# Differential attention in small blocks: steps of a pair spread over one round more, older pairs first

## The chip, the cores and the metric

The kernel runs on one core of one Trainium2 chip (trn2). It is one launch that computes a whole small network. The metric is the time of the program on the device, in microseconds (us); several runs are made, and the median is compared. A profiled execution of the same program gives the trace from which the views below come.

The engines are TensorE (PE, its weight loads are listed as PEld), VectorE (DVE), ScalarE (ACT), GpSimd (POOL) and SyncE (SP, which issues DMAs). They run side by side, each takes its own instructions in the order of the program, and they wait for each other at semaphores.

## The reference

The input is x, 2 sequences of 1024 tokens with 256 features, in float32. Eight residual layers follow each other:

```python
x = x + L0_attn_a(norm(x));  x = x + L0_ffn(norm(x))
x = x + L0_attn_b(norm(x));  x = x + L0_ffn(norm(x))
x = x + L1_attn_a(norm(x));  x = x + L1_ffn(norm(x))     # the stage of the change
x = x + L1_attn_b(norm(x));  x = x + L1_ffn(norm(x))
```

The stage of the change is the third pair. `L1_attn_a` is differential attention with 16 heads of 16 features, 4 key heads, and a softmax over the difference of two softmaxes:

```python
energy = einsum('bqhad,bkhad->bahqk', qd, kd)            # a = 0, 1
energy = where(causal, NEG, energy)
scores = softmax(energy / sqrt(D))
diff = scores[:, 0] - lam * scores[:, 1]
diff = softmax(where(causal, NEG, diff))
att = einsum('bhqv,bvhd->bqhd', diff, v)
att = att * rsqrt(mean(att * att) + EPS) * rms_w * (1 - LAM_INIT)
out = att.reshape(b, s, E) @ Wo
```

`L1_ffn` is a gated network of width 2048, `(gelu(x @ Wg.T) * (x @ Wu.T)) @ Wd.T`, with tanh gelu.

## The kernel before, in words

The function `attn_d_ffn1` computes this third pair of layers. The queries are taken in eight blocks of 128 tokens, i = 0 to 7, in both sequences (b = 0, 1). A causal block i has keys up to (i + 1) x 128. Blocks 0 to 3 have at most 512 keys and are called small, blocks 4 to 7 large. In each block and sequence the 16 heads are taken as eight pairs of heads. There are 8 x 2 x 8 = 128 pairs, the first 64 of them in small blocks.

A pair goes through these steps (functions in `attn_d_block`):

- `scores` (L1178): PE multiplies queries and keys, four matmuls into the two PSUM tiles `e` (two buffers, so one pair at a time; a large pair does it in two parts).
- `highest` (L1189): DVE adds the mask, writes the negated scores to SBUF tiles `p`, and takes the extreme value of each row into `nm`.
- `exponentials` (L1200): ACT takes exp in place with the row sums `sm`, four instructions.
- `ratio` (L1208, L1209 on DVE; L1213, L1217 on POOL): a reciprocal and a product on DVE, then POOL scales the second softmax and masks its diagonal block.
- `difference` (L1226 on DVE; L1229, L1230 on POOL): DVE adds the two and takes the row maximum `md`; POOL negates it and subtracts it.
- `turn` (L1237 on PE, L1241 on ACT), once for each head: PE transposes the blocks into the PSUM tile `dT` (one buffer), ACT takes the exp into `pT`.
- `weigh` (L1254), for every second pair: PE multiplies with the values into `py`; after the last pair of a block DVE transposes it (L1263).

The loop over rounds n in `attn_d_ffn1` starts pair n in round n, takes ratio and difference of pair n-1, the turn of pair n-2 and the weighing of pair n-3. The order within a round is written by hand: the engines PE, DVE, ACT and POOL keep the order in which the code issues (`in_order`).

Between these steps the round takes "fill" steps from the table `at`, in three portions. They are the inputs of the next block (layer norm stats, rows, turn; `queries`, `keys` and their transposes), the output of the last one (`squares`, `root`, `normalize`, `project`), and the feed-forward network (FFN) of the last block: stats, rows, turn, eight `gate` steps (L1387 on PE, a copy L1393 on ACT), `gelu` (L1398, one ACT instruction over 4096 columns), eight `up` steps (L1387, product L1395 on DVE) and eight `down` steps (L1404 on PE). For block i they fall, counted from round 16(i+1): squares 2, root 3, normalize 4, project and stats 5, rows 6, turn 7, gate 8 to 11, gelu 11, up 13 to 16, down 17 to 20. Queries and keys of the next block are made in round 12 for b = 0 and in round 15 for b = 1.

While blocks are small, `bank` alternates between two PSUM banks for gates, products and projections; in large blocks there is one.

Of the kernel before, what the change touches and what calls it, by code (L numbers as in the profile page):

```python
# [10 lines left out]
F32 = mybir.dt.float32  # L11
I32 = mybir.dt.int32
BF16 = mybir.dt.bfloat16
AF = mybir.ActivationFunctionType
# [7 lines left out]
P = 128  # L22
NTT = NT // P
NB = T // P
# [20 lines left out]
class Net:  # L45
# [899 lines left out]
    def attn_d_ffn1(self, w, wo, cos, sin, nlam, rms_w, deq):  # L945
# [5 lines left out]
        nc, tc = self.nc, self.tc  # L951
        NH, NKV, D = 16, 4, 16
        with ExitStack() as ctx:
# [33 lines left out]
            at, pairs = {}, []  # L987
# [4 lines left out]
            for i in range(NB):  # L992
                n = 16 * i
                tile_ = type("tile", (), {})()
                blocks = [
                    self.attn_d_block(pools, tile_, b, i, kT[b], v[b]) for b in range(B)
                ]
                for m, step in zip(
                    (-9, -8, -6, -4, -4, -2, -2, -2, -1, -1, -1, -1, -1),
                    (*self.attn_d_inputs(ps, work, tile_, i), *blocks[0][0], *blocks[1][0]),  # L1000
                ):
                    add(n + m if i else -1, step)
                for _, units in blocks:
                    pairs.extend(units)

                n += 16
                squares, root, normalize, project = self.attn_d_out(ps, work, tile_, wo, i)
                if i == NB - 1:

                    for m, step in enumerate((squares, root, normalize, project)):  # L1010
                        add(n + 2 + m, step)
                    continue
                stats, rows, turn, gate, gelu, up, down = self.ffn1_parts(ps, work, i, deq)
                for m, step in (
                    (2, squares), (3, root), (4, normalize), (5, project), (5, stats), (6, rows),
                    (7, turn), *((8 + k // 2, gate[k]) for k in range(8)), (11, gelu),
                    *((13 + k // 2, up[k]) for k in range(8)),
                    *((17 + k // 2, down[k]) for k in range(8)),
                ):
                    add(n + m, step)  # L1020
            nothing = type("nothing", (), {"large": False})()

            def pair(n):
                return pairs[n] if 0 <= n < len(pairs) else nothing

            def do(u, name, *args):
                f = getattr(u, name, None)
                if f:
                    f(*args)

            for step in at[-1]:
                step()
            for n in range(max(at) + 1):
                if n == 16 * 4:

                    self.ps.release()
                    self.ps = tc.alloc_tile_pool(name="d_ps1", bufs=1, space=PSUM)
                    self.small = False
                fill = at.get(n, [])
                k = (len(fill) + 2) // 3, (2 * len(fill) + 2) // 3  # L1040
                u, last, turned, weighed = (pair(n - j) for j in range(4))
                do(u, "scores", 0)
                do(u, "highest", 0)
                if not u.large:
                    do(u, "exponentials")
                do(weighed, "weigh")
                do(last, "ratio")
                for step in fill[: k[0]]:
                    step()
                do(turned, "turn", 0)  # L1050
                if u.large:
                    u.scores(1)
                    u.highest(1)
                for step in fill[k[0] : k[1]]:
                    step()
                do(turned, "turn", 1)
                if u.large:
                    u.exponentials()
                do(last, "difference")
                for step in fill[k[1] :]:  # L1060
                    step()
            self.ps.release()
# [22 lines left out]
    def attn_d_block(self, pools, tile_, b, qb, kT, v):  # L1085
# [52 lines left out]
        def pair(t, s):  # L1138
# [55 lines left out]
                if j == 1:  # L1194
                    nc.vector.tensor_tensor(own.nm, own.nm, nm, ALU.min)

            def exponentials():
                for h in range(2):
                    for a in range(2):
                        nc.scalar.activation(  # L1200
                            own.p[h][a], own.p[h][a], AF.Exp,
                            bias=own.nm[:, h, a : a + 1], scale=-1.0,
                            accum_out=own.sm[:, h, a : a + 1],
                        )

            def ratio():

# [24 lines left out]
            def turn(h):  # L1232
                dT = self.ps.tile(
                    [P, 512 if self.small else 1024], F32, tag="dT", name="dT"
                ).rearrange("p (n q) -> p n q", q=P)
                for kb in range(qb + 1):
                    nc.tensor.transpose(  # L1237
                        dT[:, kb, :], own.p[h][0][:, kb * P : (kb + 1) * P], self.ident
                    )
                pT = work.tile([P, NB, P], F32, tag="pT", name="pT", bufs=4)  # L1240
                nc.scalar.activation(pT[:, 0 : qb + 1, :], dT[:, 0 : qb + 1, :], AF.Exp)  # L1241
                shared[t, s + h] = pT

# [120 lines left out]
    def ffn1_parts(self, ps, work, i, deq):  # L1364
# [31 lines left out]

        def gelu():
            nc.scalar.activation(f.inter, f.inter, AF.Gelu_apprx_tanh)  # L1398

        def down(b, quarter):  # L1400
            if b == quarter == 0:
# [658 lines left out]
```

## Time and profile before

| what | value |
|---|---|
| median of 3 runs | 3041.03 us (3031.7 to 3042.51) |
| the profiled execution | 3038.91 us |
| its span, first to last instruction | 3037.2 us |
| busy over the span | PE 85%, DVE 64%, ACT 44%, POOL 34% |
| small blocks of the stage | 1066.8 to 1478.4 us |
| large blocks of the stage | 1478.4 to about 2174 us |
| PE busy in the small blocks, i = 0, 1, 2, 3 | 38.2, 75.0, 97.6, 106.1 us |
| mean granted TensorE clock | 0.901 |

The windows view gives the busy time of each engine in a stretch, and in brackets how many instructions started there. The wait view has one line for a pair of waiter and releaser: engine and line that waited, what it waited for, the total in us, how often, and the longest. In the timeline a line is the start, the length, the engine, the line of the code, the operation, what it writes and reads, and in square brackets the idle time before it and what ended it. A busy PE is not PE at its peak, because the ends of matmuls are modelled.

### The profile page before, as it was taken

How to read it: one execution, taken by the hardware profiler on the slowest of the kernel's cores; microseconds unless marked ns; L12 is line 12 of the kernel's file. 1: busy time of each engine (PE TensorE's matmuls, PEld its weight loads, DVE VectorE, ACT ScalarE, POOL GpSimd, SP SyncE). 2: the span in 40 equal slices, each digit the busy share in tenths (PEclk: the TensorE clock that was granted, in tenths of full speed). 3: DMA queues.
4: the chain of work that ended last, by engine and by line, in shares of the span. 5: the costliest groups of instructions: out<-in, count | busy, mean ns of one | idle time of the engine just before them, and what ended most of it. 6: DMA issues, size and time to landing. Idle time of an engine off the chain costs nothing.

```text
span 3037.2 us, 66929 instructions
## 1 busy us (share of the span) xinstructions
PE 2585.5 (85%) x26384; PEld 1608.0 (53%) x26384; DVE 1953.5 (64%) x6736; ACT 1324.4 (44%) x2672; POOL 1039.6 (34%) x1672
## 2 busy tenths in 40 slices
PE   6999998999988757887878878878777988898988
PEld 2333344434434434565655555555555767677777
DVE  5777665766664456667776858678656656566552
ACT  2776840454453256465564556656622112112110
POOL 3445232212114466566665646556500000000000
PEclk8999997999999867898989888898988889999999
DMA  3000000000001000000000000000001101101100
GB/s 115 1 1 1 1 1 1 1 1 1 1 17 40 28 1 1 1 1 1 1 1 1 1 1 1 1 1 1 18 17 24 24 20 20 23 11 36 24 9 14
DMA packets 61979, 35.39 MB, mean 12 GB/s; under 512 B 43216, under 2 KB 58080, under 8 KB 61664
## 3 DMA queue, kind: packets, MB, share of 16 engines
q1 hardware_dynamic: 59472, 29.49, 3.7%
q8 instruction: 208, 3.41, 0.4%
q10 hardware_dynamic: 2192, 1.61, 0.2%
q14 instruction: 107, 0.88, 0.1%
HBM read 22.68 MB, written 8.39 MB: 10 GB/s over the span
## 4 chain that ended last, share of the span: by engine, by line
PE 38%; DVE 13%; ACT 7%; issue 4%; POOL 3%; DMA 0%; POOLq 0%; ACTq 0%; DVEq 0%
PE ph L1387 6%; PE po L1894 5%; PE pg L1881 4%; ACT p L1200 4%; PE e L1178 4%; DVE p L1189 4%; PE pu L1881 4%; PE dT L1237 3%; PE po L1404 2%; DVE p L1226 2%; POOL p L1213 1%; PE py L1254 1%; PE pq L1564 1%; PE kh L1564 1%; PE pa L1564 1%
## 5 line engine op out<-in xcount | busy, mean ns | idle before, releaser
L1189 DVE CUSTOM_DVE_ANT_0 p<-e,mask 128x512 f32<-128x512 f32 (+3 forms) x768 | 381.6, 553 | 108.9 <-PE e L1178 107.7
L1200 ACT ACTIVATE p<-p,nm 128x128 f32<-128x128 f32 (+7 forms) x512 | 389.9, 764 | 97.4 <-DVE nm L1189 88.1
L1213 POOL TENSOR_SCALAR p<-p,ra,neg_lam 128x128 f32<-128x128 f32 (+7 forms) x256 | 221.8, 866 | 238.1 <-DVE ra L1209 178.6
L1237 PE MATMUL dT<-ident,p 128*128 128x128 f32 x1152 | 198.7, 306 | 114.4 <-ACT pT L1241 32.0
L1241 ACT ACTIVATE pT<-dT 128x128 f32<-128x128 f32 (+7 forms) x256 | 165.4, 646 | 283.5 <-PE dT L1237 282.2
L196 POOL TENSOR_SCALAR ln_mv<-ln_mv 128x2 f32<-128x2 f32 x56 | 17.6, 315 | 730.0 <-DVE ln_mv L194 720.0
L1178 PE MATMUL e<-kT,qT 32*128 32x512 f32 (+3 forms) x1536 | 235.4, 628 | 28.4 <-DVE nm L1189 27.0
L1226 DVE CUSTOM_DVE_ANT_0 p<-p,rs 128x128 f32<-128x128 f32 (+7 forms) x256 | 207.7, 832 | 70.1 <-POOL p L1217 69.8
L1237 PEld LDWEIGHTS dT<-ident,p 128*128 128x128 f32 x1152 | 153.5, 157 | 173.6 <-POOL p L1217 51.4
L845 ACT ACTIVATE pr<-s 128x512 f32<-128x512 f32 (+3 forms) x384 | 157.3, 497 | 162.9 <-PE s L840 154.2
L1230 POOL TENSOR_SCALAR p<-p,md 128x128 f32<-128x128 f32 (+7 forms) x256 | 208.8, 816 | 25.4
L550 ACT ACTIVATE pr<-s 128x1024 f32<-128x1024 f32 (+1 forms) x192 | 145.3, 812 | 131.3 <-PE s L544 83.7
L1894 PE MATMUL po<-down,inter 128*128 128x256 f32 x576 | 164.8, 451 | 3.4 <-issue 2.2
L805 PE MATMUL s<-kT,qT 32*128 32x512 f32 (+3 forms) x768 | 155.3, 518 | 3.8 <-DVE q_pad L813 1.9
L1881 PE MATMUL pg<-xT,gate 128*128 128x256 f32 x576 | 151.5, 409 | 6.5 <-ACT xT L225 5.5
L555 ACT ACTIVATE pr<-pr 128x1024 f32<-128x1024 f32 (+1 forms) x192 | 152.1, 852 | 0.0
L813 DVE CUSTOM_DVE_ANT_0 masked<-s,mask 128x128 f32<-128x128 f32 (+3 forms) x256 | 110.6, 487 | 58.9 <-PE s L805 58.8
L1894 PEld LDWEIGHTS po<-down,inter 128*128 128x128 f32 x576 | 129.8, 230 | 27.8 <-issue 2.3
L558 POOL TENSOR_SCALAR_AFFINE_SELECT pr<-pr 128x256 f32<-128x256 f32 x128 | 90.1, 721 | 154.7 <-ACT pr L555 57.7
L1881 PE MATMUL pu<-xT,up 128*128 128x256 f32 x576 | 139.3, 386 | 0.0
L1887 DVE TENSOR_TENSOR inter<-inter,pu 128x512 f32<-128x512 f32 x72 | 49.3, 685 | 133.9 <-PE pu L1881 133.9
L1387 PE MATMUL ph<-xT,gate 128*128 128x256 f32 x448 | 121.0, 417 | 10.3 <-ACT xT L225 10.1
(313 smaller groups left out, 5398.4 us busy)
## 6 DMA issues: line engine op xcount, KB each, us to landing
uk_d<-uk SPq DMA_DIRECT2D x128, 32.0 KB, 1.9
r<-uk_d SPq DMA_DIRECT2D x8, 512.0 KB, 3.9
x<-in_L_attn_a_X SPq DMA_DIRECT2D x4, 512.0 KB, 6.1
qh_d<-qh SPq DMA_DIRECT2D x8, 256.0 KB, 2.6
o<-qh_d SPq DMA_DIRECT2D x128, 16.0 KB, 1.7
out<-x SPq DMA_DIRECT2D x4, 512.0 KB, 3.1
w<-in_L_ffn_W2T SPq DMA_DIRECT2D x1, 1024.0 KB, 7.8
pk<-in_L_ffn_gate_packed SPq DMA_DIRECT2D x8, 128.0 KB, 2.4
```

What stands on the lines that cost most here:

```text
L845: nc.scalar.activation(pr[:, g, off:512], tiles[g][:, 0:m], AF.Exp, scale=0.25)
L1178: nc.tensor.matmul(own.tiles[h][:, a, 0 : hi - lo], made["q"][r : r + 32, a, t, :], kT[r : r + 32, a, lo:hi], start=True, stop=True,)
L1189: nc.vector.tensor_tensor_reduce(own.p[h][a][:, lo:hi], own.tiles[h][:, a, 0 : hi - lo], neg_row[:, T - nk + lo : T - nk + hi], -1.0, 3e38 ...
L1200: nc.scalar.activation(own.p[h][a], own.p[h][a], AF.Exp, bias=own.nm[:, h, a : a + 1], scale=-1.0, accum_out=own.sm[:, h, a : a + 1],)
L1213: nc.gpsimd.tensor_scalar(p1, p1, own.ra[:, h : h + 1], nlam[:, head : head + 1], ALU.mult, ALU.mult)
L1226: nc.vector.tensor_tensor_reduce(p0, p0, p1, own.rs[:, h, 0:1], -3e38, ALU.add, ALU.max, md)
L1230: nc.gpsimd.tensor_scalar(p0, p0, md, 1.0, ALU.add, ALU.mult)
L1237: nc.tensor.transpose(dT[:, kb, :], own.p[h][0][:, kb * P : (kb + 1) * P], self.ident)
L1241: nc.scalar.activation(pT[:, 0 : qb + 1, :], dT[:, 0 : qb + 1, :], AF.Exp)
L1387: nc.tensor.matmul(ph[:, j, :], w[:, kc, m * P : (m + 1) * P], f.xT[:, kc, :], start=(kc == 0), stop=(kc == 1),)
L1881: nc.tensor.matmul(ph[:, j, :], m_[:, kc, m * P : (m + 1) * P], f.xT[:, kc, :], start=(kc == 0), stop=(kc == 1),)
L1894: nc.tensor.matmul(f.po[:, b], inter[m // 2][:, m % 2, b * P : (b + 1) * P], wd[:, m % 2, (m // 2) * C : (m // 2 + 1) * C], start=(m == 0) ...
```

## The change

In small blocks (rounds 0 to 63) a pair's steps are spread over one round more: ratio of n-1, difference of n-2, turn of n-3, weighing of n-4. Within a round the order on every engine is: scores of n, difference of n-2, ratio of n-1, first turn of n-3, weighing of n-4, gelu if it is due, maxima and exponentials of n, half of the fill, second turn of n-3, the other half. Both heads of a pair share one `pT` tile. The FFN steps of blocks 0, 1 and 2 come one round later. In all blocks gelu is due one round later than that (12 instead of 11), and is issued after the first turn, apart from the other fill. The last small pair keeps the lags of the large ones. In large rounds the order is as before except for gelu.

```diff
                 stats, rows, turn, gate, gelu, up, down = self.ffn1_parts(ps, work, i, deq)
+                n += 1 if i < 3 else 0
                 for m, step in (
                     (2, squares), (3, root), (4, normalize), (5, project), (5, stats), (6, rows),
-                    (7, turn), *((8 + k // 2, gate[k]) for k in range(8)), (11, gelu),
+                    (7, turn), *((8 + k // 2, gate[k]) for k in range(8)), (12, gelu),
...
+            first_large = 16 * 4
+            ratios, differences, turns, weighings = {}, {}, {}, {}
+            for m, u in enumerate(pairs):
+                a, b = (2, 3) if m < first_large - 1 else (1, 2)
+                for steps, lag in (
+                    (ratios, 1), (differences, a), (turns, b), (weighings, b + 1)
+                ):
+                    steps.setdefault(m + lag, []).append(u)
...
-                fill = at.get(n, [])
-                k = (len(fill) + 2) // 3, (2 * len(fill) + 2) // 3
-                u, last, turned, weighed = (pair(n - j) for j in range(4))
-                do(u, "scores", 0)
-                do(u, "highest", 0)
-                if not u.large:
-                    do(u, "exponentials")
-                do(weighed, "weigh")
-                do(last, "ratio")
+                fill = [step for step in at.get(n, []) if not hasattr(step, "long")]
+                long = [step for step in at.get(n, []) if hasattr(step, "long")]
+                k = (len(fill) + 2) // 3, (2 * len(fill) + 2) // 3, (len(fill) + 1) // 2
+                u = pairs[n] if n < len(pairs) else nothing
+                if n < first_large:
+                    u.scores(0)
+                    do(differences, n, "difference")
+                    do(ratios, n, "ratio")
+                    do(turns, n, "turn", 0)
+                    do(weighings, n, "weigh")
+                    for step in long:
+                        step()
+                    u.highest(0)
+                    u.exponentials(0)
+                    u.exponentials(1)
+                    for step in fill[: k[2]]:
+                        step()
+                    do(turns, n, "turn", 1)
+                    for step in fill[k[2] :]:
+                        step()
+                    continue
+                if u.large:
+                    u.scores(0)
+                    u.highest(0)
+                do(weighings, n, "weigh")
+                do(ratios, n, "ratio")
                 for step in fill[: k[0]]:
                     step()
-                do(turned, "turn", 0)
+                do(turns, n, "turn", 0)
+                for step in long:
+                    step()
...
-                pT = work.tile([P, NB, P], F32, tag="pT", name="pT", bufs=4)
+                if large or h == 0:
+                    own.pT = work.tile([P, NB, P], F32, tag="pT", name="pT", bufs=4)
+                pT = own.pT if large else own.pT[:, 4 * h : 4 * h + 4]
...
+        gelu.long = True
```

More of the change, by code (lines that the diff above doesn't have):

```diff
@@ L1021, in attn_d_ffn1, with do @@
             nothing = type("nothing", (), {"large": False})()
[L1023 to L1029, printed above, removed]
+            first_large = 16 * 4
[6 more added lines that the diff above has]
+                    steps.setdefault(m + lag, []).append(u)
+            def do(steps, n, name, *args):
+                for u in steps.get(n, []):
+                    f = getattr(u, name, None)
+                    if f:
+                        f(*args)
             for step in at[-1]:
                 step()
-            for n in range(max(at) + 1):
-                if n == 16 * 4:
+            for n in range(max(max(at), max(weighings)) + 1):
+                if n == first_large:
                     self.ps.release()
@@ L1055, in attn_d_ffn1 @@
                     step()
-                do(turned, "turn", 1)
+                do(turns, n, "turn", 1)
                 if u.large:
-                    u.exponentials()
-                do(last, "difference")
+                    u.exponentials(0)
+                    u.exponentials(1)
+                do(differences, n, "difference")
                 for step in fill[k[1] :]:
@@ L1195, in highest, with exponentials @@
                     nc.vector.tensor_tensor(own.nm, own.nm, nm, ALU.min)
[L1197 to L1204, printed above, removed]
+            def exponentials(h):
+                for a in range(2):
+                    nc.scalar.activation(
+                        own.p[h][a], own.p[h][a], AF.Exp,
+                        bias=own.nm[:, h, a : a + 1], scale=-1.0,
+                        accum_out=own.sm[:, h, a : a + 1],
+                    )
             def ratio():
```

## Prediction

> **What bounds the kernel now.** I read the windows view first, cut at the rounds of the differential-attention stage (a round runs from the first scores matmul, L1178, of one pair of heads to that of the next). The 64 rounds of small blocks last from 1066.8 to 1478.4 us, 411.6 us; the four windows are the blocks i = 0 to 3, the fifth is the large blocks.
>
> ```profile
> core 0: us, PE busy (x) PEld busy (x) DVE busy (x) ACT busy (x) POOL busy (x), PEclk, DMA share, GB/s
> 1066.80:1131.70 64.90, 38.16 (x249) 22.07 (x248) 36.83 (x248) 36.77 (x165) 45.41 (x131) 0.61 0.00 1
> 1131.70:1230.80 99.10, 74.95 (x465) 48.69 (x465) 63.43 (x291) 57.29 (x181) 59.18 (x142) 0.77 0.00 1
> 1230.80:1346.30 115.50, 97.63 (x641) 67.42 (x640) 78.00 (x295) 67.59 (x180) 70.66 (x144) 0.85 0.00 1
> 1346.30:1478.40 132.10, 106.11 (x741) 71.12 (x740) 91.50 (x297) 77.19 (x180) 82.82 (x146) 0.90 0.00 1
> 1478.40:2174.00 695.60, 571.98 (x4368) 385.93 (x4369) 521.36 (x1718) 404.49 (x700) 404.33 (x557) 0.88 0.00 1
> ```
>
> No engine fills a window: POOL is the busiest at i = 0 with 45.4 of 64.9 us, PE after that with 75, 98 and 106 of 99, 116 and 132. Over the four the best engine leaves 65 + 99 + 116 + 132 - (45 + 75 + 98 + 106) = 88 us. The wait view of these 411.6 us says who waits:
>
> ```profile
> ACT p L1200 <- DVE nm L1189: 88.1, 59, 5.0
> DVE p L1226 <- POOL p L1217: 64.3, 74, 1.6
> POOL p L1213 <- DVE ra L1209: 59.7, 40, 4.6
> ```
>
> The second and third are one ring. The timeline of a round without other work (round 6, 1086.27 to 1089.80, 3.53 us) shows it:
>
> ```profile
> 1087.77 0.28 DVE L1189 CUSTOM_DVE_ANT_0 p<-e,mask 128x128 f32<-128x128 f32 x1
> ...
> 1087.98 0.17 DVE L1208 RECIPROCAL rs<-sm 128x4 f32<-128x4 f32 x1
> 1088.19 0.16 DVE L1209 TENSOR_TENSOR ra<-sm,rs 128x2 f32<-128x2 f32 x1
> ...
> 1088.53 0.44 POOL L1213 TENSOR_SCALAR p<-p,ra,neg_lam 128x128 f32<-128x128 f32 x1 [0.55 <-DVE ra L1209]
> 1089.05 0.29 POOL L1217 TENSOR_SCALAR_AFFINE_SELECT p<-p 128x128 f32<-128x128 f32 x1
> ...
> 1089.37 0.36 DVE L1226 CUSTOM_DVE_ANT_0 p<-p,rs 128x128 f32<-128x128 f32 x1 [1.02 <-POOL p L1217]
> ...
> 1090.28 0.35 DVE L1226 CUSTOM_DVE_ANT_0 p<-p,rs 128x128 f32<-128x128 f32 x1 [0.55 <-POOL p L1217]
> ```
>
> DVE finishes the maxima, makes the ratio, POOL scales and masks, and DVE waits 1.02 + 0.55 us for that before its difference and before the next round's maxima. DVE works about 1.9 us and POOL 2.63; neither runs beside the other for long, so the round takes 3.53.
>
> **What the Trainium skill says.** "Perfetto Trace Analysis", Identifying Performance Opportunities: take the most occupied engine of a regime, and ask what ends its gaps; matmul busy time is a poor measure for TensorE. The trace agrees: a full PE round (round 25, 4.73 us) shows PE busy 100% while lighter, starved ones also show high digits. "SBUF — State Buffer", Who interferes with whom: a VectorE instruction with two SBUF inputs contends with a GpSimd one that reads SBUF. The trace shows it: L1213 at 512 columns takes 0.76 us alone and 1.27 beside a difference (L1226), while L1226 keeps its 0.76. "TensorE: Matmul & The Clock Gate", Part 1: after an idle window of about 3.4 us the clock is halved. Here eight matmuls after a 5.26 us wait took 3.78 us against 1.99. "ScalarE: Activation LUTs", What ACT_TABLE_LOAD costs: 1283 ns a load, and the trace has 1.28.
>
> **The change part by part.** Counted by engine in the two programs, no instruction is added or removed: 14147 on PE, 6739 on DVE, 2179 on ACT with 18 table loads, 1678 on POOL, in each. No DMA is moved. So the sum is over order alone.
>
> Cost of a pair's steps, from the mean occupied time of their rows at i = 0, 1, 2, 3. DVE: maxima 0.85, 1.38, 1.91, 2.45; ratio 0.3 each; difference 0.70, 0.98, 1.20, 1.45. POOL: ratio (L1213, L1217) 1.54, 1.80, 2.07, 2.40; difference (L1229, L1230) 1.09, 1.35, 1.73, 2.06. ACT: exponentials 1.58, 2.02, 2.43, 2.85; pT 0.52, 0.72, 0.92, 1.11. PE: scores 0.52, 0.65, 0.90, 1.10; turn 0.30, 0.56, 0.84, 1.12; weigh, every second round, 0.40 to 1.0. Fill: each gate, up or down step 1.93 on PE with 0.5 ACT or 0.66 DVE; gelu 1.28 + 3.62 + 1.28 = 6.2 ACT; queries 0.9 PE, 0.9 DVE, 1.7 POOL; keys 0.4, 0.9, 1.1; root 2.7 and normalize 1.8 DVE; project 1.9 PE.
>
> I put each step into its round, before and after, and took the fullest engine of each round. Example: round 6 is POOL, 1.54 + 1.09 = 2.63 (measured 3.53). Round 25 (two gates) is PE, 0.65 + 0.56 + 2 x 1.93 = 5.07 (4.73: already full). Round 37 (project, stats) is DVE, 5.2, and took 10.08. Sums by block before: 48.9, 85.3, 102.9, 113.2 = 350, against the measured 411.6: **61 us are not work of the fullest engine**. About 40 lie in rounds without a gate, up or down step, 23 in those with one; the gelu pairs of rounds hold none. The same sums after: 47.8, 84.1, 103.5, 113.6 = 349. The shift of FFN steps by a round is thus free in work; what it can bring is the 61.
>
> 1. Difference two rounds behind, first on DVE and on POOL. In round n DVE takes the difference of n-2, whose mask POOL made in round n-1; POOL then has the md and p of n-2 to do while DVE makes the ratio of n-1. The ring is cut: POOL runs on without gap where it is fullest. A light round falls from 3.53 to about 2.7, 0.85 us for each of some ten at i = 0. Queued behind the difference on DVE are ratio and maxima; scores (0.5 to 1.1 us) run on PE beside them, so the maxima wait little.
> 2. Turn of n-3 right after the scores on PE, weigh of n-4 after it: their inputs are from earlier rounds, so PE's wait for POOL (48.8 + 25.4 + 24.3 us in the view) goes mostly. The pT tile for both heads lets two pairs more wait; it costs nothing.
> 3. Maxima later in DVE's round, by difference plus ratio, 1.0 to 1.75 us; exponentials and the gate copies follow. Covered in an FFN round by PE's 5.1 to 6.1 us: at i = 3 maxima end about 1.2 + 2.45 or, after an up, 2.45 + 2.45 = 4.9 us into 5.8, before the next scores need the e tiles. That cover is thin.
> 4. Gelu one round later, a round without FFN matmuls, between the pT of the two heads. ACT still needs about 9 us in that round; PE idles some 6 and starts at half clock. I take 2 us left over for each of three, 6 us, and 1.5 for each of the four rounds that hold queries, keys and their turns at once, 6 us: DVE, POOL and PE follow each other there as before.
> 5. Large blocks: order kept but for gelu. Now:
>
> ```profile
> 1589.15 3.62 ACT L1398 ACTIVATE inter<-inter 128x4096 f32<-128x4096 f32 x1
> ...
> 1594.92 1.30 PE L1237 MATMUL dT<-ident,p 128*128 128x128 f32 x5 [4.38 <-ACT v L1119]
> ...
> 1596.26 0.70 ACT L1241 ACTIVATE pT<-dT 128x640 f32<-128x640 f32 x1 [1.38 <-PE dT L1237]
> ```
>
>    After, the first pT frees dT ahead of gelu, so the second turn runs beside gelu and the 1.38 goes; gelu starts about 0.9 later. I take 1 us gained for each of four (bounds -1 and +2.5). Rounds 64 and 65 hold two differences and two turns: POOL 6.5 of 7.24 us, so nothing.
>
> Sum: small blocks 349 + 12 = 361, 50 less; large blocks 4 less; 54 in all. The profiled execution took 3038.9 us (span 3037.2), the median of the runs is 3041.0, so 2985 against the one and **2987 against the other**.
>
> **The rivals.**
> A, likeliest (0.60): as above, 2987, its own range 2968 to 3003.
> B, rounds overlap further (0.15). Two neighbours averaged, the fullest engine sums to 332: 79 + 4 saved, 2958. For it: DVE and POOL are light in PE's full rounds. Against: one set of e tiles and one dT tie neighbours together.
> C, the wait only moves (0.10). Half of the 61 stays, as DVE waiting for the mask made late behind POOL's fill, or two SBUF readers on DVE and POOL blocking each other: 31 saved, about 3010.
> D, slower (0.10). The FFN rounds, full on PE today, lose their cover: maxima are late by difference plus ratio, mean 1.5 us, PE waits for e tiles or a bank of gates, in 30 rounds 45 us, against at most 32 won in the others. It decides from 1.1 us a round; at the full 1.5 the time is 3054. Against: step 3's cover; for it: its margin at i = 3 is 0.9 us.
> E, nothing (0.05): PE is the true bound and the idle shown is its own pipeline; about 3038.
>
> **How the numbers follow.** A measurement of this kernel tells about 0.5%, 15 us, from no change. Faster by more: A, B and nearly all of C, 0.84; within: E and the rest of C, 0.06; slower: D, 0.10. The range 2956 to 3030 leaves out D, E and the third of B that goes beyond 2956.
>
> **What would show it.** Right: windows of the small blocks about 52, 88, 106 and 115 us; the wait of L1226 for L1217 down from 64 us to under 15; light rounds near 2.7 us with POOL full; FFN rounds as long as now; the project rounds 37 and 53 (then 38 and 54) at 6 to 7 us. Wrong: FFN rounds over 6.5 us with PE waiting for nm (L1189 of after) or for gate copies; the fifth window off by over 8 us.

## The result, and the profile after

The changed kernel takes 3024.86 us in the median (3017.52 to 3034.71, 20 runs), the kernel before 3035.89 us in the same comparison (20 runs): a ratio of 0.996, 95% interval 0.995 to 0.997. It is faster by 11 us where 54 were forecast. The profiled span is 3024.8 us, at a mean granted clock of 0.904.

Cut at four marks (first scores of round 0, first scores of round 64, start of the last weighing matmul, end), the two profiled executions are:

| stretch | before, us | after, us | forecast of the difference |
|---|---|---|---|
| ahead of the stage | 1066.8 | 1067.7 | 0 |
| small blocks, rounds 0 to 63 | 411.6 | 400.9 | -50 |
| large blocks | 716.4 | 712.4 | -4 |
| the rest | 842.4 | 843.8 | 0 |

So nearly the whole miss is in the small blocks. The windows view of the changed kernel, cut at its own rounds 0, 16, 32, 48 and 64:

```profile
core 0: us, PE busy (x) PEld busy (x) DVE busy (x) ACT busy (x) POOL busy (x), PEclk, DMA share, GB/s
1067.70:1131.50 63.80, 44.51 (x247) 27.20 (x246) 35.15 (x244) 36.26 (x163) 44.38 (x127) 0.55 0.00 1
1131.50:1230.40 98.90, 80.43 (x447) 51.24 (x446) 60.75 (x289) 56.90 (x180) 59.50 (x143) 0.71 0.00 1
1230.40:1343.70 113.30, 98.10 (x639) 68.18 (x638) 75.91 (x295) 67.15 (x180) 68.90 (x143) 0.88 0.00 1
1343.70:1468.60 124.90, 107.10 (x735) 72.64 (x735) 90.32 (x297) 77.13 (x180) 79.05 (x143) 0.90 0.00 1
1468.60:2160.50 691.90, 569.45 (x4394) 383.61 (x4395) 525.40 (x1726) 405.39 (x702) 407.29 (x560) 0.90 0.00 1
```

The four windows lost 1.1, 0.2, 2.2 and 7.2 us, where about 13, 11, 10 and 17 were forecast. The wait view of the small blocks of the changed kernel (waiter and what it waited for; us in total, times, longest) says that waits went and others came:

```profile
POOL md L1259 <- DVE md L1256: 65.6, 24, 7.7
ACT pT L1274 <- PE dT L1267: 63.8, 65, 2.3
ACT v L1150 <- DVE rope L268: 40.0, 8, 6.2
ACT p L1230 <- DVE nm L1220: 39.6, 42, 2.4
...
DVE p L1256 <- POOL p L1247: 27.3, 42, 1.8
PE dT L1267 <- ACT pT L1274: 26.1, 22, 5.4
...
PE e L1209 <- DVE nm L1220: 15.1, 18, 1.5
```

The fifth of these is the ring of before (L1226 for L1217), down from 64.3 us to 27.3. PE's own wait for POOL's mask (25.4 us before, beside 48.8 on its weight loads) is gone from the top of the list; 12.1 us on the weight loads are left. The exponentials' wait for the maxima fell from 88.1 to 39.6. What is new is POOL's wait for DVE's md, 65.6 us in only 24 waits where it was 11.9, and ACT's wait ahead of its copy of v, 40.0 us in eight waits where it was 14.1. Few and long waits belong to single rounds, not to every round.

The times of the rounds say which. Light rounds fell from 3.53 us to 2.83 to 3.12 (rounds 3 to 8). Round 5 (1080.42 to 1083.54), beside round 6 of before in the prediction, shows that DVE's waits for the mask are no longer 1.02 and 0.55 us but 0.57 and 0.55:

```profile
1081.34 0.35 DVE L1256 CUSTOM_DVE_ANT_0 p<-p,rs 128x128 f32<-128x128 f32 x1 [0.57 <-POOL p L1247]
...
1082.25 0.35 DVE L1256 CUSTOM_DVE_ANT_0 p<-p,rs 128x128 f32<-128x128 f32 x1 [0.55 <-POOL p L1247]
```

FFN rounds without queries and keys, apart from the first gate rounds, are on average as long as before or shorter: rounds 26 and 27 are 5.12 and 5.46 us (before 5.89 and 4.73), rounds 49 and 50 are 6.32 and 5.34 (6.09 and 6.67). But round 30 takes 15.59 us, round 46 15.86 and round 62 15.75; round 25 takes 9.83, 41 9.96, 57 10.39; and round 15 takes 10.65.

To compare with the forecast I take each round's length less its fullest engine, by the sums of the prediction (349 us in all), and add them up by kind of round:

| kind of round | rounds | forecast, us | after | gelu_before_v | combo_spread | warm_rounds_before |
|---|---|---|---|---|---|---|
| last gates, gelu, first ups | 28-30, 44-46, 60-62 | 6 | 16.2 | -1.3 | 4.2 | 5.8 |
| all input steps of a sequence | 15, 31, 47, 63 | 6 | 17.7 | 17.6 | -1.5 | -1.8 |
| first two gates | 25, 41, 57 | 0 | 11.1 | 11.2 | 12.2 | 8.4 |
| projection | 22, 38, 54 | 0 | 7.9 | 8.0 | 7.5 | 6.8 |
| light | 1-11 | 0 | 5.6 | 5.5 | 5.4 | 5.5 |
| other input rounds | 12-14 | 0 | 5.3 | 5.2 | 5.8 | 5.8 |
| the others | | 0 | -11.9 | -13.4 | -13.2 | -12.4 |
| sum | | 12 | 51.9 | 32.8 | 20.4 | 18.1 |

The last three columns are experiments told of below. "The others" is negative because the sums charge a full FFN round a little more than it takes. The sums are those of the changed kernel in each column: what an experiment moves between rounds, or adds, is not in them.

### The profile page after: what moved, and what is told of

Its sections match the earlier page's. It is cut to its first block, busy times and chain, and to the rows that moved or that the text cites. A ratio compares the mean times of both kernels' runs of the same rounds, so it can differ in the third digit from the quotient of the medians.

```text
span 3024.8 us, 66879 instructions
## 1 busy us (share of the span) xinstructions
PE 2592.0 (86%) x26384; PEld 1613.2 (53%) x26384; DVE 1949.4 (64%) x6736; ACT 1324.3 (44%) x2672; POOL 1037.1 (34%) x1672
## 4 chain that ended last, share of the span: by engine, by line
PE 38%; DVE 13%; ACT 7%; issue 5%; POOL 3%; DMA 0%; POOLq 0%; ACTq 0%; DVEq 0%
PE ph L1420 6%; PE po L1929 5%; PE pg L1916 4%; PE pu L1916 4%; ACT p L1230 4%; PE e L1209 3%; DVE p L1220 3%; PE dT L1267 3%; PE po L1439 2%; DVE p L1256 2%; PE py L1287 2%; PE pq L232 1%; POOL p L1243 1%; PE pq L1599 1%; PE kh L1599 1%
## 5 line engine op out<-in xcount | busy, mean ns | idle before, releaser
L1230 ACT ACTIVATE p<-p,nm 128x128 f32<-128x128 f32 (+7 forms) x512 | 389.7, 764 | 51.3 <-DVE nm L1220 39.6
L1209 PE MATMUL e<-kT,qT 32*128 32x512 f32 (+3 forms) x1536 | 243.9, 607 | 44.9 <-DVE nm L1220 43.3
L196 POOL TENSOR_SCALAR ln_mv<-ln_mv 128x2 f32<-128x2 f32 x56 | 18.1, 324 | 728.4 <-DVE ln_mv L194 718.4
L1256 DVE CUSTOM_DVE_ANT_0 p<-p,rs 128x128 f32<-128x128 f32 (+7 forms) x256 | 206.4, 832 | 32.0 <-POOL p L1247 31.9
L1260 POOL TENSOR_SCALAR p<-p,md 128x128 f32<-128x128 f32 (+7 forms) x256 | 207.0, 809 | 25.4
L1420 PE MATMUL ph<-xT,up 128*128 128x256 f32 x448 | 126.2, 433 | 27.5 <-DVE inter L1428 20.5
L1209 PEld LDWEIGHTS e<-kT,qT 32*128 32x128 f32 x1536 | 91.9, 213 | 103.4 <-DVE nm L1220 74.1
L1259 POOL TENSOR_SCALAR md<-md 128x1 f32<-128x1 f32 x256 | 90.9, 355 | 161.4 <-DVE md L1256 149.6
```

The source lines that it names most:

```text
L1209: nc.tensor.matmul(own.tiles[h][:, a, 0 : hi - lo], made["q"][r : r + 32, a, t, :], kT[r : r + 32, a, lo:hi], start=True, stop=True,)
L1230: nc.scalar.activation(own.p[h][a], own.p[h][a], AF.Exp, bias=own.nm[:, h, a : a + 1], scale=-1.0, accum_out=own.sm[:, h, a : a + 1],)
L1256: nc.vector.tensor_tensor_reduce(p0, p0, p1, own.rs[:, h, 0:1], -3e38, ALU.add, ALU.max, md)
L1260: nc.gpsimd.tensor_scalar(p0, p0, md, 1.0, ALU.add, ALU.mult)
L1420: nc.tensor.matmul(ph[:, j, :], w[:, kc, m * P : (m + 1) * P], f.xT[:, kc, :], start=(kc == 0), stop=(kc == 1),)
```

## The experiments

Two theories were set up from the trace. **Q** (queue): what stands ahead of gelu in ACT's order sets when gelu starts. The timeline of the changed kernel, PE and ACT from the end of round 28 to round 30 (round 29 begins at 1197.82):

```profile
1195.34 0.59 ACT L1426 COPY inter<-ph 128x512 f32<-128x512 f32 x1 [0.58 <-PE ph L1420]
...
1197.07 0.81 PE L232 MATMUL pkv<-wd,xT 128*128 128x192 f32 x4
...
1200.66 0.21 ACT L1150 COPY v<-pkv 128x64 f32<-128x64 f32 x1 [4.45 <-DVE rope L268]
1200.77 0.39 ACT L1274 ACTIVATE pT<-dT 128x256 f32<-128x256 f32 x1
1201.17 1.28 ACT L1431 ACT_TABLE_LOAD   x1
...
1202.47 3.62 ACT L1431 ACTIVATE inter<-inter 128x4096 f32<-128x4096 f32 x1
...
1206.10 1.28 ACT L1230 ACT_TABLE_LOAD   x1
1207.40 0.51 ACT L1230 ACTIVATE p<-p,nm 128x256 f32<-128x256 f32 x1
...
1209.38 0.36 ACT L1274 ACTIVATE pT<-dT 128x256 f32<-128x256 f32 x1
1209.88 0.66 PE L1267 MATMUL dT<-ident,p 128*128 128x128 f32 x2 [5.37 <-ACT pT L1274]
```

Gelu's input is complete at about 1195.9, with the last gate copy. ACT then waits 4.45 us, because the copy of v, a fill step of round 28, is next in its order and starts only when DVE's rope of the keys has ended. The product that it copies, `pkv`, had left PE at 1197.88 already; the rope reads the same tile, and why the copy waits for it the trace doesn't say. Gelu starts 6.5 us after the last gate copy, of which its table load is 1.28. The load, itself and the load back (6.2 us) then stand ahead of the exponentials of the pair and of the second pT, and PE waits 5.37 us for that pT. The Trainium skill says in "TensorE: Matmul & The Clock Gate", Architectural detail (the paragraph on queue depths), that ACT and DVE take their instructions strictly first in, first out; these lines show it, with 4.45 us of ACT behind a copy of 0.21.

In the kernel before, the same place reads:

```profile
1195.54 0.59 ACT L1393 COPY inter<-ph 128x512 f32<-128x512 f32 x1 [0.38 <-PE ph L1387]
...
1196.43 1.28 ACT L1398 ACT_TABLE_LOAD   x1
1197.02 1.98 PE L232 MATMUL pq<-wd,xT 128*128 128x512 f32 x4
1197.73 3.62 ACT L1398 ACTIVATE inter<-inter 128x4096 f32<-128x4096 f32 x1
...
1204.90 0.19 ACT L1119 COPY v<-pkv 128x64 f32<-128x64 f32 x1
1205.14 0.66 PE L1237 MATMUL dT<-ident,p 128*128 128x128 f32 x2 [5.26 <-ACT v L1119]
```

There gelu starts 1.6 us after the last gate copy, the copy of v comes behind it, and PE's wait behind gelu is much the same, 5.26 us.

**C** (clock; the prediction's rival C is another): the half clock of PE makes the rounds longer. The rival to both was that the new order is worth little and the long rounds are its price.

**gelu_before_v.** Gelu of the small blocks is put back straight behind the last gate copies, ahead of the copy of v.

```diff
-                    (7, turn), *((8 + k // 2, gate[k]) for k in range(8)), (12, gelu),
+                    (7, turn), *((8 + k // 2, gate[k]) for k in range(8)), (11 if i < 3 else 12, gelu),
...
-        gelu.long = True
+        if i >= 3:
+            gelu.long = True
```

> The changed kernel with one edit: in blocks 0 to 2 gelu is issued right after the last gate copy (round 12 of the shifted FFN, as fill) and so ahead of the copy of v on ACT; in the changed kernel it stands a round later, behind that copy. Theory Q (queue): in the changed kernel ACT idles 4.45 us before gelu in round 29 because the copy of v waits for the keys' rope on DVE, which waits for POOL; so gelu starts some 4 to 5 us earlier here, the span of rounds 28 to 31 falls from 39.7 to about 35, and the same at rounds 44 to 47 and 60 to 63: 12 us less than the changed kernel, a ratio to the kernel before of about 0.992. Rival R (empty round): what hurts is only that any gelu blocks exponentials and dT for 9 us whatever stands around it; then the time stays within 4 us of the changed kernel, ratio 0.995 to 0.997.

Measured: 3001.82 us, ratio to before 0.9898 (0.9885 to 0.991), small blocks 381.8 us. Its timeline at the same place (round 29 begins at 1196.33):

```profile
1193.85 0.58 ACT L1426 COPY inter<-ph 128x512 f32<-128x512 f32 x1 [0.58 <-PE ph L1420]
1193.87 1.88 PE L232 MATMUL pq<-wd,xT 128*128 128x512 f32 x4
1194.45 1.28 ACT L1431 ACT_TABLE_LOAD   x1
1195.58 0.81 PE L232 MATMUL pkv<-wd,xT 128*128 128x192 f32 x4
1195.74 3.62 ACT L1431 ACTIVATE inter<-inter 128x4096 f32<-128x4096 f32 x1
...
1200.67 0.38 ACT L1274 ACTIVATE pT<-dT 128x256 f32<-128x256 f32 x1
...
1200.95 0.21 ACT L1150 COPY v<-pkv 128x64 f32<-128x64 f32 x1
1201.20 0.66 PE L1267 MATMUL dT<-ident,p 128*128 128x128 f32 x2 [4.16 <-ACT v L1150]
```

Gelu now runs beside the projection of queries and keys and beside DVE's rope, the copy of v no longer waits, and rounds 29 and 30 take 7.10 and 8.10 us instead of 4.78 and 15.59. PE still waits 4.16 us behind gelu: the line names the copy of v, which ended last; the pT that frees `dT` ended 0.11 us earlier. Of the 19.1 us that the small blocks lose, 17.5 are in these rounds: the first row of the table falls from 16.2 to -1.3. Q holds, and its size was more than expected. But the edit does two things at once: it takes gelu from behind the copy, and it puts it a round earlier, beside the projection.

**v_copy_on_dve.** Gelu stays in its new place and only the copy of v leaves ACT, for the keys of small blocks.

```diff
-            nc.scalar.copy(
+            (nc.scalar.copy if large else nc.vector.tensor_copy)(
                 v[:, qb, :, 0:D], pkv[...]
```

> The changed kernel with one edit: in small blocks the copy of v out of PSUM is made by DVE and not by ACT; gelu keeps its round (29, 45, 61) and its place after the first turn. Theory Q (what stands ahead of gelu in ACT's order sets its start): the 4.45 us in which ACT waits ahead of the copy go, gelu of round 29 starts about 3 us earlier, and 6 to 10 us are saved over the three: a ratio to before of 0.993 to 0.994, rounds 28 to 31 about 3 us shorter in sum. Rival R (a round without FFN matmuls is the loss, wherever ACT is held): the time stays that of the changed kernel, ratio 0.996.

Measured: 3018.86 us, ratio 0.9942 (0.9928 to 0.9955), small blocks 394.2 us, 6.7 less. In round 29 (from 1195.85):

```profile
1197.03 0.38 ACT L1274 ACTIVATE pT<-dT 128x256 f32<-128x256 f32 x1 [2.79 <-PE dT L1267]
1197.43 1.28 ACT L1431 ACT_TABLE_LOAD   x1
...
1206.14 0.66 PE L1267 MATMUL dT<-ident,p 128*128 128x128 f32 x2 [3.35 <-ACT pT L1274]
```

The load for gelu comes 1.6 us after the round's start where it came 3.35 after it; rounds 30 and 46 lose 2.7 and 2.8 us. The edit reaches only these two of the three places: the keys that are made in round 60 are those of block 4, a large one, so their copy of v stays on ACT and holds gelu as before. The timeline of round 61 (from 1423.95):

```profile
1426.79 0.21 ACT L1150 COPY v<-pkv 128x64 f32<-128x64 f32 x1 [4.48 <-DVE rope L268]
1426.90 0.60 ACT L1274 ACTIVATE pT<-dT 128x512 f32<-128x512 f32 x1
1427.52 1.28 ACT L1431 ACT_TABLE_LOAD   x1
```

Round 62 loses nothing there (15.83), which makes this place a control. Q holds. In rounds 28 to 30 and 44 to 46 the edit takes off 5.0 us where gelu_before_v takes off 11.6, so the copy is about two fifths of that gain. The rest I put down to gelu running beside PE's projection there, where PE has work; that share was not measured by itself.

**keys_own_rope** and **before_rope_own.** The rope of the keys uses the same SBUF tiles as that of the queries, so DVE waits until POOL has summed those. The edit gives the keys tiles of their own, once in the changed kernel, once in the kernel before.

```diff
-                [(out[..., 0:NKV, :], view)], "rq",
+                [(out[..., 0:NKV, :], view)], "rq" if heads == NH else "rk",
```

> The changed kernel with one edit: the keys' rope gets SBUF tiles of its own, so DVE need not wait for POOL to read the queries' rope before it writes the keys'. Theory: the wait of the keys' rope (11.6 us in 8 times, about 1.4 each) goes, and with it a part of the wait of the copy of v (40 us in 8 times) and of gelu behind it; the gain is 8 to 14 us over the changed kernel, ratio to before about 0.992. Rival: POOL is the next in the chain (queries' product 1.27 us, then keys'), the keys' rope is early and then waits in POOL's queue, and only 0 to 4 us come back, ratio 0.995 to 0.996.

> The kernel before with one edit: tiles of their own for the rope of the keys. In the changed kernel this saved 11 us. Theory Q: the wait of the keys' rope for POOL was there before too, but gelu stood ahead of the copy of v that waits for it, so it held less: at most 5 us, ratio 0.998 to 1.0. Rival: the ring costs the same with or without the change (11 us, ratio 0.9965), and the change did not make it worse.

Measured: in the changed kernel 3013.45 us, ratio 0.9931 (0.9914 to 0.9948), small blocks 387.9, that is 13.0 less; in the kernel before 3037.94 us, ratio 1.0007 (0.9997 to 1.0016). The same wait was in both kernels (12.8 us of DVE before, 11.6 after). Taking it away brought nothing in the kernel before, where gelu was ahead of the copy that hangs on it, and 13 us in the changed kernel, where gelu is behind. This supports Q: the change did not add this wait. The two kernels differ in more than gelu's place, though; combo, below, says how much of the 13 us is gelu's.

**lags_alone.** The changed kernel with the order of before within small rounds; lags, places of the FFN and gelu stay.

```diff
                 if n < first_large:
                     u.scores(0)
-                    do(differences, n, "difference")
-                    do(ratios, n, "ratio")
-                    do(turns, n, "turn", 0)
-                    do(weighings, n, "weigh")
-                    for step in long:
-                        step()
                     u.highest(0)
                     u.exponentials(0)
                     u.exponentials(1)
+                    do(weighings, n, "weigh")
+                    do(ratios, n, "ratio")
+                    for step in fill[: k[0]]:
+                        step()
+                    do(turns, n, "turn", 0)
+                    for step in long:
+                        step()
...
```

The difference follows last, after the second turn.

> The changed kernel with one edit: the lags (difference of n-2, turn of n-3), the FFN shift and gelu's place stay, but in small rounds the order is that of before (scores, maxima, exponentials, weigh, ratio, fill in thirds around the turns, difference last). Theory O (order matters): DVE's difference then stands behind the first two thirds of the fill, yet maxima come first again, and PE and ACT get work early in the FFN rounds; light rounds stay short since the ring is cut by the lag alone, so light rounds about 3 us. If the order of the changed kernel is what makes DVE and PE take turns in rounds with fill, this is faster than the changed kernel by 5 to 20 us, ratio 0.990 to 0.994. Rival: the older pair's step first is needed for the gain; then light rounds go back to 3.5 us and the ratio is 0.997 to 1.003.

Measured: 3026.04 us, ratio 0.9976 (0.9966 to 0.9986), small blocks 402.1. That is what the changed kernel takes, but made up otherwise:

| rounds | lags_alone, us | after, us |
|---|---|---|
| 0-11 | 39.1 | 36.6 |
| 12-15 | 25.7 | 27.2 |
| 16-23 | 41.7 | 33.5 |
| 24-31 | 58.0 | 65.4 |
| 32-39 | 48.1 | 44.4 |
| 40-47 | 63.4 | 68.9 |
| 48-55 | 56.0 | 49.4 |
| 56-63 | 70.3 | 75.4 |

The light rounds are back at 3.6 us: a round more between the steps does nothing without the older pair's step first. And the order gains 21 us in the stretches without gelu and gives 19.5 back in those with gelu or with the heavy input rounds, where the exponentials of lags_alone stand ahead of gelu. Of the 19.5, 7.5 us are in the first gate rounds 25, 41 and 57. This is where the forecast gain went. The new order without the lag was not run.

**combo.** gelu_before_v and keys_own_rope together (both diffs above).

> Both edits that have gained alone: gelu straight after the last gate copies (round 28, 44, 60) and tiles of their own for the rope of the keys. If the two waits are separate, the gains over the changed kernel add up (20 and 11 us): a ratio to before of 0.987. If the rope's wait cost time mostly because the copy of v stood ahead of gelu, the second edit brings little once gelu is ahead of it: ratio 0.989, and the small blocks take about 380 us as with gelu moved alone (381.8).

Measured: 3000.7 us, ratio 0.9879 (0.9862 to 0.9895), small blocks 376.8. The second edit brings 5.0 us here where it brought 13.0 alone: between the two expectations. By difference some 8 of its 13 us hung on gelu's place, and the rest lies elsewhere.

**combo_spread.** combo with the inputs of the next block spread over a round more: the turns of the first sequence in round 13 instead of 14, queries and keys of the second in 14 instead of 15.

```diff
-                    (-9, -8, -6, -4, -4, -2, -2, -2, -1, -1, -1, -1, -1),
+                    (-9, -8, -6, -4, -4, -3, -3, -3, -2, -2, -1, -1, -1) if i <= 4 else
+                    (-9, -8, -6, -4, -4, -2, -2, -2, -1, -1, -1, -1, -1),
```

> The kernel called combo with one edit: for small blocks and the first large one the inputs of the next block are spread over one round more: the turns of the first sequence a round earlier, queries and keys of the second in round 14 and only its turns in round 15 (counted in 16s). Theory H (the chain queries, rope, sum on POOL, turn, kT follows itself in one round, and the next pair's difference stands behind its last step on DVE): the rounds 15, 31, 47 and 63, which take 4 to 5 us more than their fullest engine, lose 2.5 to 4 us each, round 14 gains under 1 each: 8 to 14 us less than combo, ratio 0.983 to 0.986. Rival (the excess there is PE and DVE work in any case, or moves into round 14 with its two up steps): within 3 us of combo.

Measured: 2992.8 us, ratio 0.9855 (0.9841 to 0.9868), small blocks 369.4. Why a round with all five input steps is long is seen in combo's round 15 (1118.87 to 1129.02), read by the idle time in the brackets:

```profile
1120.61 3.78 PE L232 MATMUL pq<-wd,xT 128*128 128x512 f32 x4
...
1124.43 0.69 DVE L259 TENSOR_TENSOR rope<-pq,rope_d 128x512 f32<-128x512 f32 x1 [3.17 <-PE pq L232]
...
1125.93 1.26 POOL L273 TENSOR_TENSOR qr<-rope,rope 128x512 f32<-128x512 f32 x1 [3.04 <-DVE rope L268]
...
1127.24 0.66 PE L1159 MATMUL t_ps<-ident,qr 128*128 128x128 f32 x4 [1.57 <-POOL qr L273]
...
1129.13 0.61 DVE L1167 TENSOR_SCALAR kT<-t_ps,half 128x128 f32<-128x128 f32 x2 [2.87 <-PE t_ps L1165]
...
1130.09 0.23 POOL L1259 TENSOR_SCALAR md<-md 128x1 f32<-128x1 f32 x1 [1.65 <-DVE md L1256]
```

PE, DVE, POOL, PE and DVE again each wait for the one before, and because the last step (kT) is the end of DVE's round, the next pair's difference stands behind it and POOL waits for that. Part of this round is clock too: the first line takes 3.78 us, while in round 28 of gelu_before_v the same four matmuls take 1.88, and in round 15 of the kernel before they took 1.98. In rounds 31, 47 and 63 they take 1.88. With the chain spread over rounds 14 and 15 round 15 falls from 10.15 to 5.92 us, 31 from 11.66 to 7.25, 47 from 12.20 to 8.05 and 63 from 13.89 to 9.72. Rounds 13, 29, 45 and 61, which take the turns of the first sequence, give back 1.3 to 2.4 us each. The net is 7.4 us in the trace; the ratio falls by 0.0024, about 7 us, a little under the 8 to 14 that were expected.

**warm_pe** and **warm_rounds_before.** Eight idle matmuls in each of some rounds keep PE busy. In warm_pe they are added to the changed kernel in rounds 22 to 25, 38 to 41 and 54 to 57; in warm_rounds_before they are added to combo_spread, and not in the gate rounds 25, 41 and 57. `WARM` is (6, 7, 8, 9) in the first and (6, 7, 8) in the second.

```diff
+                    if n >= 18 and n % 16 in WARM:
+                        idle = self.bank(ps, "idle")
+                        for _ in range(8):
+                            nc.tensor.matmul(
+                                idle[:, 0:P], self.ident, self.ident,
+                                start=True, stop=True,
+                            )
                     u.highest(0)
```

> The changed kernel with one addition: eight matmuls of the identity with itself in each of rounds 6 to 9 (counted modulo 16, from round 22 on), in the middle of PE's round, into a bank that nobody reads. They compute nothing that is used. Theory C (clock): in the changed kernel PE runs at half clock in these lightly loaded rounds, and the first gate round (25, 41, 57) takes 9.8 to 10.4 us with scores at 1.92 instead of 0.71 us and eight gate matmuls at 3.75 instead of 1.99; with PE kept busy it takes about 6.5, 3 to 4 us less at each of three places, so 8 to 10 us less than the changed kernel in all, less what the additions cost: ratio about 0.993. Rival: the additions (about 1.2 us a round warm, 2.4 cold) lengthen these rounds by as much as they warm, or DVE's chain ahead sets the first gate round; then the time is the same or up to 8 us longer, ratio 0.996 to 0.999.

> The kernel called combo_spread with eight idle matmuls (the identity with itself, the result unused) after the weighing of rounds 22, 23 and 24 (and 38 to 40, 54 to 56), none in the gate rounds themselves. Theory C (half clock sets the first gate round): rounds 25, 41 and 57 fall from 10.4 to about 7 us, the first eight gate matmuls from 3.78 to 1.9; the idle matmuls cost about 2 us in the three rounds ahead; 3 to 5 us less in all, ratio 0.984. Rival (the clock falls again between, or the round waits for something else): these rounds stay at 10 us, the kernel is 6 us longer than combo_spread, ratio 0.9875.

Measured: warm_pe 3027.54 us, ratio 0.9982 (0.9973 to 0.9991), small blocks 401.4: no gain. Its round 25 holds 3.02 us of idle matmuls and takes 10.71, so what the clock gave was spent again (the eight take 1.95 us at full clock, where 1.2 were expected). warm_rounds_before 2986.0 us, ratio 0.9831 (0.9809 to 0.9853), small blocks 367.1. The first gates of round 25, in combo_spread:

```profile
1163.68 1.92 PE L1210 MATMUL e<-kT,qT 32*128 32x256 f32 x8 [0.53 <-DVE nm L1221]
...
1167.89 3.78 PE L1421 MATMUL ph<-xT,gate 128*128 128x256 f32 x8
```

and in warm_rounds_before:

```profile
1166.51 1.40 PE L1220 MATMUL e<-kT,qT 32*128 32x256 f32 x8 [0.52 <-DVE nm L1231]
...
1170.02 1.99 PE L1431 MATMUL ph<-xT,gate 128*128 128x256 f32 x8
```

The same eight matmuls take 1.99 us instead of 3.78, and round 25 falls from 10.46 to 7.38, round 57 from 10.50 to 9.06. The granted clock rose from 0.57 to 1.00 of full in round 25 and from 0.69 to 1.00 in round 57. Round 41 does not fall (10.34 and 11.04): there the clock was 0.69 on average, as it was 0.64 without, although it was 1.00 in rounds 36 to 40 just before; why it fell is open. The idle tile also takes a turn of the two PSUM banks, so the gates of rounds 25 and 57 come to the other bank and those of round 41 don't; this was not separated. So half clock accounts for most of what makes rounds 25 and 57 long, but idle matmuls are a poor cure: 2.3 us net in the trace, and the intervals of the two ratios overlap.

**rows_later** and **rows_and_warm.** combo_spread with the rows of the next block's layer norm a round later, alone and with the idle matmuls.

```diff
-                    (-9, -8, -6, -4, -4, -3, -3, -3, -2, -2, -1, -1, -1) if i <= 4 else
+                    (-9, -7, -6, -4, -4, -3, -3, -3, -2, -2, -1, -1, -1) if i <= 4 else
```

> The kernel called combo_spread with one edit: for small blocks the rows of the next block's layer norm (nine small DVE instructions of 1.9 us in sum, two POOL ones of 1.1) are made a round later, in round 25 (41, 57) and not in round 24 (40, 56). Theory T (the first gate round is late because DVE's difference and maxima stand behind these rows at the end of round 24): rounds 24 and 25 lose 2 us together, three times, 6 us: ratio to before 0.9835. Rival C (round 25 is PE at half its clock: eight gate matmuls 3.78 us): the rows hide in either round, within 2 us of combo_spread, ratio 0.985 to 0.986.

> combo_spread with both edits, rows a round later and idle matmuls in rounds 22 to 24 and so on. If T and C both hold, about 10 us less than combo_spread, ratio 0.982. If the clock alone is the limit, as warm_rounds_before within 2 us.

Measured: rows_later 2992.86 us, ratio 0.9855 (0.9832 to 0.9878), small blocks 369.4, as combo_spread to the tenth. Theory T is out: the rows hide in either round. rows_and_warm 2992.11 us, ratio 0.984 (0.9814 to 0.9866), small blocks 366.2: as the idle matmuls alone, within what can be told.

**gelu_old_place_all.** The changed kernel with gelu in its old place in all eight blocks, to isolate step 5 of the prediction, gelu in large blocks.

```diff
-                    (7, turn), *((8 + k // 2, gate[k]) for k in range(8)), (12, gelu),
+                    (7, turn), *((8 + k // 2, gate[k]) for k in range(8)), (11, gelu),
...
-        gelu.long = True
```

> The changed kernel with gelu in its old place in all eight blocks, straight after the last gate copies, in large blocks too; rounds and lags as changed. Step 5 of the prediction (in large blocks the new place of gelu gains about 1 us each of four): the large stage goes back from 691.9 to about 695.6 us, the small blocks take 381.8 as with gelu moved there alone, ratio to before 0.991. Rival (the 3.7 us of the large blocks come from elsewhere, as the rounds where the lags change): the large stage stays at 691.6 to 692, ratio 0.9898.

Measured: 3008.79 us, ratio 0.9914 (0.9893 to 0.9934); small blocks 381.8, as forecast; large blocks 718.8 us against 714.5 with gelu's new place (gelu_before_v). The direction is that of step 5 and the size is near 4, but it can't be called shown: the ratios' intervals overlap, and among the kernels of the study with gelu's new place this stretch lasts 710.0 to 716.8 us, while the three with its old place (before_rope_own, the kernel before and this one) have 713.1, 716.4 and 718.8.

A kernel with the new order and the old places of the output and FFN steps was not run: squares and what follows read what the last weighing of a block leaves, and with the lag of four that comes in round 3 of the next block, so those steps have to come a round later too.

## Why the prediction was wrong, point by point

The direction was right and the size was not: 11 us where 54 were forecast. The failed part is the term "12 us left over" for the small blocks, which measured 52.

**Step 1 (ring cut) held for the most part.** Light rounds take 2.83 to 3.12 us where 2.7 was forecast. L1256's wait for POOL's mask came down to 27.3 us and not under 15. In light rounds POOL is nearly full and DVE's difference meets its mask just in time (waits of 0.55 to 0.57 us), so that remaining wait costs little: 5.6 us over rounds 1 to 11. lags_alone showed that the lag without the order does not do this.

**Step 2 (PE's waits for POOL) held**: they left the top of the list. PE's next wait is for ACT's pT, 26.1 us with a longest of 5.4, and it belongs to step 4.

**Step 3 (the cover of FFN rounds) held**, but for the first gate rounds. The other FFN rounds without queries and keys are on average not longer than before, up to i = 3. Rival D, which needed them 1.1 us longer, is excluded. The sign named for it, PE waiting for the maxima, did come: 15.1 us in 18 waits, the last line of the wait view. None of them falls in those full FFN rounds; they are in rounds without gates, ups or downs, in rounds 30, 46 and 62 behind gelu, and, with 0.5 to 1.4 us each, in the first gate rounds, which at 9.8 to 10.4 us are also over the 6.5 named there.

**Step 4 (gelu, and the heavy rounds) failed.** I worked out rightly that ACT needs about 9 us and that PE idles some 6 at the cost of its clock, and then took 2 us left over for each gelu. It was 16.2 over three, 5.4 each (an estimated 0.8 of that is the misread cost below). What was missed is, for one, what stands ahead of gelu in ACT's order: the copy of v of the round before, which waits for DVE's rope. In the kernel before, gelu was issued ahead of that copy. I had moved gelu past it without counting it, and had read the wait view of before, where the copy's wait stood with 14.1 us, without asking what would now be queued behind it. gelu_before_v shows what the place costs, 17.5 us in these rounds; v_copy_on_dve gives the copy about two fifths of that at the two places it reaches; the rest I put down to the round in which gelu runs, which was not measured alone. The heavy rounds were given 1.5 us each and took 4.4 (an estimated 1.4 of it misread cost in three of them): their chain passes PE, DVE, POOL, PE and DVE in turn, so the fullest engine of the round is no measure for it, and in the new order the next pair's difference stands first behind its end on DVE. combo_spread shows it, for round 15 together with the half clock.

**A cost that was misread.** The sums charge PE 0.9 us for a sequence's queries and 0.4 for its keys. The traces show 1.88 to 1.98 and 0.81 at full clock (`pq` and `pkv` in the timelines above), about twice that. PE is the fullest engine in rounds 28, 31, 44, 47, 60 and 63, so the sum after is short by an estimated 8 to 9 us, worked out from these durations. Rounds 28, 44 and 60 hold gates and queries together only since the FFN was shifted: by the prediction's costs they add up to 20.7 us, and they took 23.2. So the shift was not free in work. In the total the opposite error offsets it, the 11.9 us by which the sums charge other rounds too much.

**A term that was missing: the first gate rounds.** They were summed at full clock. In the trace the first eight matmuls of round 25 take 3.75 us, as eight did after a wait in the prediction's own example (3.78), and the granted clock was 0.60, 0.66 and 0.69 in the three. It is 11.1 us over three; warm_rounds_before shows the clock as the main cause in two of them. Before the change it was so in part already: the first gate rounds 24, 40 and 56 took 7.26, 8.46 and 7.65 us at clocks of 0.71, 0.68 and 0.85. The new ones are 6.8 us longer in sum.

**The project rounds** fell as forecast in part: 36 to 38 from 8.71, 10.08 and 6.14 to 5.12, 6.11 and 6.97 us; round 38 is in the 6 to 7 that were forecast, round 54 with 9.11 is not.

**Step 5 (large blocks)**: 3.7 us by the windows against 4 forecast, but a single profile doesn't settle it, as said above.

**The rivals.** The time lies between C (the wait only moves, 31 us saved) and E (nothing). C is right in kind, but of the 61 us 52 stayed and not half, and the new waits are others than those it named. A's mechanism is there once the rest is mended: with gelu, the keys' rope and the inputs placed otherwise the small blocks take 369.4 us, and 367.1 with idle matmuls, against the 361 forecast. That is 42 and 44 us less than before, of the 50. Some of it may not need the change: the keys' rope brought nothing in the kernel before, but spreading the inputs was not tried there. Taken one after another the edits account for 19.1 (gelu's place), 5.0 (keys' rope), 7.4 (inputs spread) and 2.3 us (clock) of the 39.9 by which the small blocks missed the forecast; about 6 stay open, the projection rounds among them.

The fastest kernels of the study are combo_spread and those made from it: 0.9855 of the time before for combo_spread and rows_later, 0.9831 and 0.984 with idle matmuls. Their intervals overlap, and combo_spread needs no idle work.

## What to carry to other kernels

When a long instruction is moved in the order of an in-order engine, list what it is now behind and what each of these waits for: a copy of 0.21 us held a gelu of 3.62 for 4.45 us, and a wait whose removal brought nothing in the old order was worth 13 us in the new one, some 8 of them by gelu's place. A sum over rounds of the fullest engine is good for rounds whose steps are independent; where a round holds a chain over several engines, take the chain's length, or spread it over two rounds. And charge matmuls in and after starved rounds at the clock that the trace shows there, not at full clock.

## What the runs showed of the hardware that was not expected

The same program takes different times in single profiles, by stretch: the large blocks of six kernels with one and the same program there (keys_own_rope, combo, combo_spread and the three made from it) lasted 710.0 to 716.8 us, and the stretch behind the stage, in which nothing was edited in any kernel, 831.3 to 847.4 us. So a few us between two spans say little. The small blocks had to be compared by themselves: the two kernels that are the same program there, gelu_before_v and gelu_old_place_all, both took 381.8 us, and many single rounds agree to 0.02 us between kernels.
